# Recurrent layer's last slab: a separate load of the logarithm's table behind the square

## The chip, the cores and the metric

The kernel runs on one core of one Trainium2 chip. The metric is the device time of one execution in microseconds; the median of three runs is given. Engines are named as in the profile: PE is TensorE's matrix multiply and PEld its weight load, DVE is VectorE, ACT is ScalarE, POOL is GpSimd, SP is SyncE, which here issues most DMAs.

## The reference, cut to what matters

Four layers run one after the other on x of 32 sequences of 64 tokens with 256 features: a cross-attention block, two transformer decoder layers, and a recurrent layer of the RWKV kind. The change lies in the last of them. Cut to its second half, that layer computes

```python
outs = scan over 64 steps of:  out = r_t . (u * a + s);  s = a + w_t * s;  a = k_t outer v_t
att  = outs.reshape(b, l, E)
a4   = att.reshape(b, l, 32, 8)                       # 32 heads of 8
m    = mean(a4, -1);  var = mean((a4 - m) ** 2, -1)
att  = ((a4 - m) * rsqrt(var + 1e-5)) * gn_w + gn_b   # group norm over a head
x    = x + att * g @ Wo.T                             # g = silu gate
xn2  = layernorm(x);  sx2 = token_shift(xn2)
rr   = sigmoid((xn2 + sx2 * maa_r) @ ffn_Wr.T)
kk   = square(relu((xn2 + sx2 * maa_k) @ ffn_Wk.T))
x    = x + rr * (kk @ ffn_Wv.T)
```

The reciprocal square root of the group norm is the place of the change.

## The kernel before, in words

All data of the recurrent layer are kept with features on the partitions and tokens along the free axis. The 2048 tokens are cut into eight slabs n = 0 to 7 of four sequences, 256 tokens each (`RB` = 4, `RR` = 256); slab n is half u = n % 2 of group g = n // 2. A slab's work is a list of pieces in three parts, made by `recurrent` (L631):

- first: layer norm and token shift, the five mixes, the projections, the decay, the gate;
- second: the outer products and the scan on VectorE, the sum over keys, then the group norm `norm_a` (L845) and `norm_b` (L855), and the output projection Wo with `to_rows` (L870), whose result `add_to_x` (L214) adds to x;
- third: the feed-forward part: its layer norm (`norm`, L648, through `layernorm_T`, L155), the mixes `xk` and `xr` (L681), `ff_key` (L900: project, then Relu at L903 and Square at L904), the receptance projection `pfr` whose result `done_r` (L906) turns into a tanh (L909), and the value projection `pfv`, whose result `done_v` (L911) multiplies and adds on VectorE (L914, L915) and writes out by DMA (L916).

Each piece has a time written by hand (`FIRST`, `SECOND`, `THIRD`, `ENDS`, L15 to L19), in units of a slab, with slab n shifted by n. `emit` (L93) sorts the pieces of all slabs by these times and calls them, so that the third part of slabs 4, 5 and 6 lies among the second part of slab 7. The program is then ordered for each engine by a scheduler that simulates a timeline (L1268). An instruction can be pinned behind another one by `tc.issue_after`, which `at_once` (L142) uses for runs of matmuls.

The group norm in detail. `norm_a` adds the own term (L847), takes the heads' mean by two matmuls with an averaging matrix into the bank `pgm` (L850), subtracts it on VectorE (L851), and squares on ScalarE into `sq` (L853). `norm_b` takes the mean of the squares by two more matmuls into the bank `pgv` (L859). The power -1/2 is then made on ScalarE as exp(-0.5 ln(v + 1e-5)):

```python
nc.scalar.activation(ps, ps, AF.Ln, bias=tiny[:, 1:2])     # L861
nc.scalar.activation(ps, ps, AF.Exp, scale=-0.5)           # L862
```

and VectorE multiplies with scale and gate (L865, L866). The output projection `pwo` (L875) waits for that, and `add_to_x` (L216) for the projection.

ScalarE evaluates a function from a table, and a set of tables is brought in by an instruction of its own, ACT_TABLE_LOAD. These loads are not written in the kernel: they are put into ScalarE's stream ahead of an activation whose function is not in the set that is there, once the order of the stream is known. They carry the line of the activation that they serve (L861 ahead of the logarithm, L862 ahead of the exponential, L599 and L500 in the transformer layers, L794 in the decay).

The small matrices of the feed-forward part (`pln`, `pst`, `pkk`, `pfr`, `pfv`) lie in PSUM banks with the tag "tp", of which there are two, taken in turn (`BUFS`, L110); a matmul into a bank waits until the reader of what was in it before is done.

Of the kernel before, what the change touches and what calls it, by code (L numbers as in the profile page):

```python
# [33 lines left out]
AF = mybir.ActivationFunctionType  # L34
# [6 lines left out]
NG = 4  # L41
# [57 lines left out]
def tile_xattn_stack(ctx: ExitStack, tc: tile.TileContext, a: dict, out: bass.AP):  # L99
    nc = tc.nc  # L100
# [11 lines left out]
    def bank(name, tag="mm"):  # L112
        return psum.tile([P, 512], FP, tag=tag, name=name, bufs=BUFS[tag])
# [517 lines left out]
    def recurrent(n, pool, c3):  # L631
# [3 lines left out]
        st = {}  # L635
# [9 lines left out]
        def tile_(name, bufs=2, shape=None, p=pool, tag=None):  # L645
            return p.tile(shape or [P, 2, RR], FP, tag=tag or name, name=f"{name}_{t}", bufs=bufs)
# [198 lines left out]
        def norm_a():  # L845
            at = st["at"] = tile_("at")
            nc.vector.tensor_tensor(at, st["own"], st["pa"], ALU.add)  # L847
            ps = bank(f"pgm_{t}", "pc")[:, :RR]
            for c in range(2):
                nc.tensor.matmul(ps, c3["avg"], at[:, c], start=(c == 0), stop=(c == 1))  # L850
            nc.vector.tensor_tensor(at, at, ps.unsqueeze(1).broadcast_to([P, 2, RR]), ALU.subtract)  # L851
            st["sq"] = tile_("sq", 1)
            nc.scalar.activation(st["sq"], at, AF.Square)  # L853

        def norm_b():  # L855
            at, sq = st["at"], st["sq"]
            ps = bank(f"pgv_{t}", "pc")[:, :RR]
            for c in range(2):
                nc.tensor.matmul(ps, c3["avg"], sq[:, c], start=(c == 0), stop=(c == 1))  # L859

            nc.scalar.activation(ps, ps, AF.Ln, bias=tiny[:, 1:2])  # L861
            nc.scalar.activation(ps, ps, AF.Exp, scale=-0.5)  # L862
            gnh = c3["gnh"]
            for c in range(2):
                nc.vector.scalar_tensor_tensor(at[:, c], at[:, c], gnh[:, c : c + 1], ps, ALU.mult, ALU.mult)  # L865
                nc.vector.scalar_tensor_tensor(  # L866
                    at[:, c], at[:, c], gnh[:, 2 + c : 3 + c], st["gt"][:, c], ALU.add, ALU.mult
                )
# [16 lines left out]
        for fn in (spread, outer, scan, read, over_keys):  # L885
            second += [(0.5, lambda fn=fn, e=e: fn(e)) for e in range(2)]
        second += [(0.5, norm_a), (0.5, norm_b)]
        def done_o(ps):
            add_to_x(g, u, ps)
# [58 lines left out]
    with tc.tile_pool(name="lw", bufs=1) as wp, tc.tile_pool(name="lp", bufs=2) as pool:  # L948
# [157 lines left out]
        for i, L in enumerate(("L1", "L2")):  # L1106
            for k in range(2):
                for g in range(NG):
# [5 lines left out]
                    at = (8 + GAP) * i + 4 * k + g  # L1114
# [7 lines left out]
            at = (8 + GAP) * i + MLP  # L1122
# [149 lines left out]
```

## Time and profile before

| what | us |
|---|---|
| median of three runs | 1058.6 |
| the three runs | 1058.6, 1056.49, 1059.2 |
| the profiled execution's own time | 1057.36 |
| its span, from the first to the last instruction | 1055.6 |
| mean granted TensorE clock (of 1) | 0.974 |
| span from 1003 us on: length / TensorE / VectorE / ScalarE busy | 52.6 / 34.7 / 33.4 / 22.7 |
| table loads on ScalarE: number / all together | 49 / 62.9 |
| of these L861 and L862, one each in a slab | 8 and 8 |
| last output's add on VectorE (L915): start | 1051.66 |

How to read it. The share of busy time of an engine is a mean over the whole span. The chain of waits is followed back from the last instruction: at each step to what released it, or to the instruction before it on its engine; "issue" is time in which the engine waited for nothing that the profile shows. Lines of a timeline give start, duration, engine, line of the source, operation, output and inputs with their shapes, a count, and in brackets the idle time ahead of the instruction and who ended it. Starts and durations of neighbours on an engine overlap by some 0.1 us, since instructions are pipelined. Matmuls in float32 appear as two records each. In table-like lines of a group, the numbers behind the bar are busy time in us and the mean in ns of one, then the idle time ahead of it.

The names in the profile have no slab number; by the order of the program, the work from 1024 us on is that of slab 7's group norm, slab 6's layer norm (`xn_fr`, `pln_fr`, `pst_fr`), and the feed-forward parts of slab 4 (`pfr`, `pfv`, `rr` first in time), then 5, 6 and 7.

### The profile page before, as it was taken

The numbers are of one execution on the slowest core, as the hardware profiler recorded it, in microseconds if no ns is written. First come the engines' busy times: TensorE is split into PE (matmuls) and PEld (weight loads), VectorE is DVE, ScalarE is ACT, GpSimd is POOL, SyncE is SP. The second block draws the span as 40 slices with busy tenths as digits, with TensorE's granted clock in tenths as the row PEclk, the third lists the DMA queues.
The fourth block names the chain that finished last, engine by engine and source line by source line (L and its number), as shares of the span: only waits on it lengthen the run. The fifth ranks groups of instructions, "written<-read, shape, count | busy, mean of one in ns | idle before, by whom it ended". The sixth has DMA issues, their size and how long they took to land.

```text
span 1055.6 us, 25954 instructions
## 1 busy us (share of the span) xinstructions
PE 963.1 (91%) x10636; PEld 776.0 (74%) x10636; DVE 741.4 (70%) x1415; ACT 553.4 (52%) x1279; POOL 554.9 (53%) x584
## 2 busy tenths in 40 slices
PE   8999999998999999989999999997979989989757
PEld 4887787776788987967777778875857777666546
DVE  5863778787875646567777865337588786899984
ACT  4744756454466445654554575533545566355244
POOL 4343998798874347578688875130224431243300
PEclk9999999999999999999999999998989999999889
DMA  9300111111101000141101110021321304223401
GB/s 302 112 22 21 42 27 42 42 28 27 32 2 47 1 16 7 58 135 38 41 23 27 27 52 22 11 67 26 92 65 28 90 12 102 70 52 72 100 1 40
DMA packets 45945, 53.36 MB, mean 51 GB/s; under 512 B 16146, under 2 KB 40068, under 8 KB 43780
## 3 DMA queue, kind: packets, MB, share of 16 engines
q1 hardware_dynamic: 40292, 49.60, 17.6%
q10 hardware_dynamic: 5536, 2.12, 0.8%
q8 instruction: 84, 1.38, 0.5%
q14 instruction: 33, 0.27, 0.1%
HBM read 38.83 MB, written 4.21 MB: 41 GB/s over the span
## 4 chain that ended last, share of the span: by engine, by line
PE 43%; DVE 27%; POOL 14%; ACT 7%; issue 3%; DMA 3%; SPq 2%; ACTq 0%; DVEq 0%; POOLq 0%
DVE vb_r L829 7%; PE pf_L2m L205 4%; PE pfo_L1m L205 3%; PE pfo_L2m L613 3%; DVE vb_r L814 3%; POOL s_L2s L481 2%; PE pf_L1m L205 2%; POOL s_L1c L481 2%; POOL s_L2s L485 2%; PE pr L330 2%; SPq L421 2%; DVE x L216 1%; PE pwo_r L875 1%; POOL s_L1c L485 1%; PE pk_r L210 1%
## 5 line engine op out<-in xcount | busy, mean ns | idle before, releaser
L721 POOL TENSOR_TENSOR x_r<-x_r,xn_r 128x512 f32<-128x512 f32 x40 | 60.6, 1530 | 143.1 <-DVE x_r L718 131.8
L829 DVE TENSOR_TENSOR_SCAN vb_r<-wsh,vb_r 128x512 f32<-128x512 f32 x64 | 76.5, 1262 | 14.2 <-ACT wsh L725 14.2
L613 PE MATMUL pfo_L2m<-w_L,hT_L2m 128*128 128x256 f32 x256 | 61.2, 383 | 0.1
L205 PE MATMUL pfo_L1m<-w_L,hT_L1m 128*128 128x256 f32 x384 | 56.0, 292 | 4.7 <-DVE hT_L1m L605 2.1
L205 PE MATMUL pf_L2m<-lnT_L2m,w_L 128*128 128x256 f32 x384 | 55.2, 294 | 2.1 <-ACT hT_L2m L599 2.1
L205 PEld LDWEIGHTS pfo_L1m<-w_L,hT_L1m 128*128 128x128 f32 x384 | 50.5, 195 | 7.8 <-DVE hT_L1m L605 2.9
L205 PEld LDWEIGHTS pf_L2m<-lnT_L2m,w_L 128*128 128x128 f32 x384 | 49.0, 190 | 5.6 <-ACT hT_L2m L599 2.7
L613 PEld LDWEIGHTS pfo_L2m<-w_L,hT_L2m 128*128 128x128 f32 x256 | 47.0, 190 | 7.9 <-issue 1.3
L481 POOL TENSOR_TENSOR s_L2s<-s_L2s,n 128x512 f32<-128x512 f32 x32 | 41.5, 1314 | 20.9 <-DVE s_L2s L476 15.1
L205 PE MATMUL pf_L1m<-lnT_L1m,w_L 128*128 128x256 f32 x384 | 51.6, 287 | 0.1
L481 POOL TENSOR_TENSOR s_L1s<-s_L1s,n 128x512 f32<-128x512 f32 x32 | 40.5, 1282 | 19.7 <-DVE s_L1s L476 19.6
L481 POOL TENSOR_TENSOR s_L1c<-s_L1c,n_L1c 128x512 f32<-128x512 f32 x32 | 41.0, 1302 | 17.0 <-DVE s_L1c L476 16.8
L481 POOL TENSOR_TENSOR s_L2c<-s_L2c,n_L2c 128x512 f32<-128x512 f32 x32 | 40.5, 1286 | 17.6 <-DVE s_L2c L476 17.6
L205 PEld LDWEIGHTS pf_L1m<-lnT_L1m,w_L 128*128 128x128 f32 x384 | 47.8, 191 | 2.0 <-issue 1.2
L605 DVE TENSOR_TENSOR hT_L1m<-hf_L1m,hT_L1m 128x512 fp32r<-128x512 f32 x32 | 29.2, 916 | 24.6 <-POOL hT_L1m L604 24.6
L604 POOL TENSOR_SCALAR hT_L1m<-hf_L1m 128x512 fp32r<-128x512 f32 x32 | 21.4, 671 | 45.6 <-ACT hf_L1m L599 39.6
L599 ACT ACTIVATE hf_L1m<-pf_L1m,b_L 128x256 f32<-128x256 f32 x64 | 26.8, 473 | 29.1 <-PE pf_L1m L205 26.3
L599 ACT ACTIVATE hT_L2m<-pf_L2m,b_L 128x256 f32<-128x256 f32 x64 | 26.6, 472 | 29.0 <-PE pf_L2m L205 28.9
L718 DVE SCALAR_TENSOR_TENSOR x_r<-px_r,vecs,sx_r 128x256 f32<-128x256 f32 x80 | 33.5, 475 | 9.2 <-PE px_r L150 9.2
L300 ACT ACTIVATE att<-pe,nmx 128x256 f32<-128x256 f32 x64 | 29.6, 478 | 19.1 <-DVE nmx L298 16.8
L814 DVE TENSOR_TENSOR vb_r<-vb_r,rT_r 128x2048 f32<-128x2048 f32 x16 | 38.5, 2413 | 0.0
L150 PE MATMUL pa_r<-vb_r,sel 128*32 128x256 f32 x256 | 20.4, 447 | 19.2 <-DVE vb_r L814 19.2
(383 smaller groups left out, 2973.6 us busy)
## 6 DMA issues: line engine op xcount, KB each, us to landing
vb_r<-vd_r SPq DMA_DIRECT2D x16, 1024.0 KB
raw_w_L<-in_L_w_dram SPq DMA_DIRECT2D x3, 1024.0 KB
y<-in_y_dram SPq DMA_DIRECT2D x8, 256.0 KB
x<-in_x_dram SPq DMA_DIRECT2D x8, 256.0 KB
ctxT_L1c<-in_yT_dram SPq DMA_DIRECT2D x4, 512.0 KB
kbd<-kT_L1s SPq DMA_DIRECT2D x64, 32.0 KB
kbd<-kT_L1c SPq DMA_DIRECT2D x64, 32.0 KB
kbd<-kT_L2s SPq DMA_DIRECT2D x64, 32.0 KB
```

The source lines that it names most:

```text
L205: nc.tensor.matmul(ps, sta[x], mov[y], start=(at == 0), stop=(at == n - 1))
L300: nc.scalar.activation(att[:, 2 * h + c, :], pe[:, c, :], AF.Exp, bias=nmx[:, h, c : c + 1], accum_out=rs[:, h, c : c + 1],)
L481: nc.gpsimd.tensor_tensor(s[:, r], s[:, r], n(j).unsqueeze(1).broadcast_to([P, 8, S]), ALU.add)
L485: nc.gpsimd.tensor_tensor(s[:, r], s[:, r], mx[:, hs].unsqueeze(2).broadcast_to([P, 8, S]), ALU.subtract)
L599: nc.scalar.activation(raw[:, i], ps[:, i], AF.Gelu_apprx_tanh, bias=w()["b1"][:, 2 * f2 + i : 2 * f2 + i + 1])
L604: nc.gpsimd.tensor_scalar(h[:, 0], raw, 1.0, 0.0, ALU.mult, ALU.add)
L605: nc.vector.tensor_tensor(h[:, 1], raw, h[:, 0], ALU.subtract)
L613: nc.tensor.matmul(st["ps"][:, v], st["h"][:, f, rows], w2[:, f], start=(f == 0), stop=(f == 7))
L718: nc.vector.scalar_tensor_tensor(d[:, c], banks[m][:, c], vec("L3_maa_stack", 2 * m + c), sx_("x", c), ALU.add, ALU.mult)
L721: nc.gpsimd.tensor_tensor(d, d, st["x"], ALU.add)
L814: nc.vector.tensor_tensor(v, v, x.unsqueeze(1).broadcast_to([P, 4, 2 * RR]), ALU.mult)
L829: nc.vector.tensor_tensor_scan(v[:, d], flat(st["wsh"]), v[:, d], 0.0, ALU.mult, ALU.add)
```

## The change

```diff
@@ norm_a
             st["sq"] = tile_("sq", 1)
-            nc.scalar.activation(st["sq"], at, AF.Square)
+            st["squared"] = nc.scalar.activation(st["sq"], at, AF.Square).ins
 
@@ norm_b
             for c in range(2):
                 nc.tensor.matmul(ps, c3["avg"], sq[:, c], start=(c == 0), stop=(c == 1))
 
+            if n == 2 * NG - 1:
+
+                with tc.issue_after(st["squared"]):
+                    nc.scalar.preload_act_table(AF.Ln)
             nc.scalar.activation(ps, ps, AF.Ln, bias=tiny[:, 1:2])
             nc.scalar.activation(ps, ps, AF.Exp, scale=-0.5)
```

For the last slab only (n = 7), an ACT_TABLE_LOAD of the logarithm's set is written into the kernel, and pinned behind the square of the same slab. Nothing is taken out. Four lines are added ahead of L861, so a line number of the kernel before from L861 on is greater by four in the changed one (the logarithm is L865, the exponential L866, `pwo` L879, the tanh L913); the new load has L864.

The order of ScalarE's stream from that square to that exponential, in the two programs (slab numbers from the program's names):

```
before                                changed
L853 square, slab 7                   L853 square, slab 7
                                      L864 table load
L173 normalise, slab 6, x2            L173 normalise, slab 6, x2
                                      L913 table load
L909 tanh, slab 4                     L913 tanh, slab 4
L861 table load                       L865 table load
L861 logarithm, slab 7                L865 logarithm, slab 7
L862 table load                       L866 table load
L862 exponential, slab 7              L866 exponential, slab 7
```

TensorE's stream differs in one place: in the program before, the four transposes `pln` of slab 6 stand behind the first matmul of slab 7's `pwo`; in the changed one they stand ahead of all four. The other engines have the same instructions in the same order.

## The prediction

> **What bounds the kernel now.** I read the page first, for the engines' shares and the chain that ended last, then that chain in order of time for the last 40 us, then ScalarE (ACT) alone for the same stretch, and last the groups of table loads.
>
> ```profile
> span 1055.6 us, 25954 instructions
> PE 963.1 (91%) x10636; PEld 776.0 (74%) x10636; DVE 741.4 (70%) x1415; ACT 553.4 (52%) x1279; POOL 554.9 (53%) x584
> PE 43%; DVE 27%; POOL 14%; ACT 7%; issue 3%; DMA 3%; SPq 2%; ACTq 0%; DVEq 0%; POOLq 0%
> ```
>
> TensorE is busy for 91% and ScalarE for 52%. That average says nothing of the place of the edit: the last 28 us of the span are a single dependent string of small steps, in which each engine hands on to the next. The chain there:
>
> ```profile
> 1019.57 1.99 PE pwo_r L875 x8
> ...
> 1023.76 1.73 PE pfr_r L875 x8
> 1025.48 1.73 PE pfv_r L875 x8
> 1027.21 0.88 PE pgv_r L859 x4
> 1028.09 0.02 issue
> 1028.11 0.45 ACT pgv_r L861
> 1028.56 0.02 issue
> 1028.58 1.28 ACT L862
> ...
> 1029.87 0.38 ACT pgv_r L862
> ...
> 1031.60 0.70 PE pwo_r L875 x2
> 1032.29 0.44 PE pln_fr L181 x4
> 1032.73 1.31 PE pwo_r L875 x6
> ```
>
> The logarithm of slab 7 (L861, at 1028.11) starts 0.02 us after the matmuls pgv that make its input. What held it is TensorE, and not a table. From there the chain runs through logarithm, the exponential's load, exponential, VectorE, pwo and so on to the end: each microsecond by which the logarithm comes later is one at the end. ScalarE in front of it (start, duration):
>
> ```profile
> 1024.52 0.63 ACT L853 ACTIVATE sq_r<-at_r 128x512 f32<-128x512 f32 x1 [0.32 <-DVE at_r L851]
> 1025.05 1.08 ACT L173 ACTIVATE xn_fr<-x,nmr_fr,rstd_fr 128x256 f32<-128x256 f32 x2
> 1026.04 0.57 ACT L909 ACTIVATE rr_r<-pfr_r 128x512 f32<-128x512 f32 x1
> 1026.63 1.28 ACT L861 ACT_TABLE_LOAD   x1
> 1028.11 0.45 ACT L861 ACTIVATE pgv_r<-pgv_r,tiny 128x256 f32<-128x256 f32 x1 [0.20 <-PE pgv_r L859]
> ```
>
> The square, two normalisations (slab 6), the tanh of slab 4's receptance gate (L909), the logarithm's load. The load ends at 1026.63 + 1.28 = 1027.91, and ScalarE then sits idle for 0.20 us until pgv is there. So the load that the change wants to move is hidden already, with 0.20 us to spare: a perfect move is worth nothing.
>
> **The change part by part.** (1) The edit names one load more. It does not take the old one out, because the tanh stands between the square and the logarithm. In the changed program ScalarE's order is: square, load, normalisation x2, load, tanh, load, logarithm, load, exponential. The normalisations (Identity) run on whatever table is there, as they do in slab 4, where Identities stand between logarithm and exponential with a single load. The tanh does not: it needs its own table back, and the logarithm then needs its own again. So three loads stand where one stood, two more than before. Each costs 1.283 us, in all groups of them:
>
> ```profile
> L861 ACT ACT_TABLE_LOAD x8 | 10.3, 1283 | 2.5 <-DVE x L216 2.4
> L862 ACT ACT_TABLE_LOAD x8 | 10.3, 1283 | 0.1
> ```
>
> Walked forward with gaps of 0.02 us ahead of a load and 0.01 behind it (as around 1028.58): square to 1025.15; load 1025.17 to 1026.45; normalisations 1026.46 to 1027.55 (1.08 to 1.09 for two); load 1027.57 to 1028.85; tanh, whose input has been there since 1025.5, 1028.86 to 1029.45 (mean of that line 0.59); load 1029.48 to 1030.76; logarithm at 1030.77. That is 1030.77 - 1028.11 = 2.66 us late: 2 x 1.28 of loads, some 0.3 of overlaps between neighbours that the loads break up, less the 0.20 of idle time.
>
> The Trainium skill ("ScalarE: Activation LUTs", "What ACT_TABLE_LOAD costs") gives a load 1283 ns, as here, and a drain of about 1380 ns on top, 2.66 us for every switch. The rows do not show that drain: the exponential starts 0.01 us after its load. By that rule two switches would be 5.3 us and the total about 1063.5 us. The same page ("Table sets: the hidden batching unit") tells the author to do all calls of one set before switching, and that speaks against a load placed ahead of a tanh.
>
> (2) What waits behind the delayed tanh. Its bank is that of the next pkk (slab 5), in a pair of banks taken in turn, and pkk lists a wait for ScalarE. Before, pkk followed pgv at once (1028.09); now it waits for the tanh to 1029.45, an idle gap of 1.36 us on TensorE. pkk and the pfr behind it (1.73 us each) then end at about 1033.0. VectorE's L914 (slab 4's output, 1.4 us with L915) waits for the same tanh: 1029.47 to 1030.9, its DMA 2 us later. Both are covered: nothing needs them before the normalised rows reach VectorE, 1030.27 + 2.66 = 1032.93, and pwo, 1031.60 + 2.66 = 1034.26. If that cover were too short, pwo would move by the excess; 1.2 us are to spare.
>
> (3) TensorE's order changes in one place. Before, four transposes pln (0.44 us, slab 6) stood between the first pair and the other six records of pwo, so pwo lasted 1031.60 to 1034.04 = 2.44 us. In the changed program they stand ahead of all of pwo, which then lasts 1.99, as slab 6's own pwo did at 1019.57. That is 0.45 us gained on the chain, if the transposes are done by 1034.26. They need the bank that ScalarE frees with slab 5's first kk (L903), directly behind the exponential: exponential 1032.53 to 1032.90, kk to about 1033.4, transposes to about 1033.95. It fits with 0.3 us to spare. Had they to wait for slab 5's tanh instead (0.63 + 0.60 after kk), they would end at about 1035.2, and pwo would be 0.9 us late. Bounds of this step: -0.45 to +0.9 us; I take -0.45, since kk is the reader of the bank that is next in turn.
>
> All other engines have the same instructions in the same order. Behind pwo the chain has the same waits as before: VectorE's sum, statistics, Pool, and the last feed-forward.
>
> The sum: +2.66 - 0.45 = +2.2 us. The profiled execution took 1057.36 us (span 1055.6 and 1.8 around it), so 1059.6; it was 1.2 us under the median of 1058.6, against which 2.2 more is 1060.8. The three runs shown lie 2.7 us apart (1056.49 to 1059.2), 0.26%. So about 0.3% (3.2 us) is what can be told from no change, and the forecast, +0.21%, lies inside that.
>
> **The rivals.**
> *TensorE's clock falls (slower).* The clock is granted in stretches of 3.41 us:
>
> ```profile
> 198.48:201.89 3.41, 1.72 (x17) 1.00 0.16 39
> 201.89:205.30 3.41, 3.41 (x14) 0.50 0.02 5
> 317.90:321.30 3.40, 2.02 (x75) 1.00 0.09 18
> 321.30:324.70 3.40, 3.40 (x32) 1.00 0.00 0
> ```
>
> The columns are the stretch, its length, TensorE's busy time (instructions), the granted clock, the DMA's share and GB/s. A stretch with 1.72 us busy (an idle gap of 1.69) was followed by one at half clock; one with 2.02 busy (a gap of 1.38) was not. The new gap of 1.36 us, if it falls in one stretch, leaves 2.05 busy: just on the safe side. Were the gap some 0.3 us longer, the next 3.41 us would do half their work, 1.7 us late, with pkk, pfr and part of pwo in them; at most 1.2 of it is absorbed ahead of pwo, else 1.7 arrives. Added: 1.2 to 1.7, total +3.4 to +3.9, 1062.0 to 1062.5. For it: the margin is only 0.3 us and how the stretches lie to the kernel is chance. Against: the 1.38 row.
> The skill ("TensorE: Matmul & The Clock Gate", "Part 1: The HAM clock gate (the “warmup” mystery)") has the half rate only after about a whole idle window of 3.4 us; the row at 198.48 shows it after half of one, and by the page this rival would cost nothing.
>
> *The transposes come late.* The other end of step 3: 2.66 + 0.9 - 0.45 = +3.1 us, 1061.7. For it: three ScalarE instructions stand close behind the exponential. Against: the order of the banks.
>
> *The extra loads cost nothing on the path (equal or faster).* If the repeated loads were skipped because the table is there, or the tanh could move away, the logarithm would again be held by pgv and only the 0.45 of step 3 would remain: 1058.15. This is also the case in which the edit does what it says. For it: only the idle 0.20 us and the new order of pwo. Against: the changed program issues the loads, and each of 49 loads in this trace took 1.28 us, whatever stood ahead of it.
>
> **How the numbers follow.** Forecast (+2.2) 0.65; clock 0.12; late transposes 0.12; free loads 0.11. The forecast is 1.0 us under the bound of 3.2 us and the runs shown scatter by 2.7 in all, so a third of it (0.22) may be read as slower; the clock case gives 0.11 and the late transposes 0.07: slower 0.40. Faster by over 0.3% could only be scatter around the last case: 0.03. Within 0.3%: 0.57. The range: down to 1058.6 the forecast less most of the scatter, and up to 1063.4, the clock case with 0.9 of scatter; outside lie most of the free loads and the far ends of scatter.
>
> **What would show it.** In the changed profile: 51 table loads instead of 49, three of them between slab 7's square and its logarithm; the logarithm 0.01 us behind a load and no longer behind pgv; 6.2 us from the square's start to the logarithm's (before 3.6); pkk 1.3 to 1.4 us after pgv; pwo 1.99 us in one piece, 3.5 us behind the logarithm's start as before; the granted clock at 1.00 up to the end. It would be wrong if loads after a load were shorter, if pwo waited for the transposes, or if the clock fell in the last 25 us.

## The result, and the profile after

| | before | changed |
|---|---|---|
| median of 20 runs each, us | 1059.2 | 1063.16 |
| ratio of times | 1 | 1.0033 (95%: 1.0019 to 1.0048) |
| profiled execution, us | 1057.36 | 1068.0 |
| from the start of slab 7's square to the start of the last add | 27.14 | 29.37 |
| from the span's start to that square | 1024.52 | 1032.88 |

By the ratio the changed kernel is slower by 3.5 us (2.0 to 5.1) in 1059; the two medians lie 3.96 us apart. The stretch that the prediction argued about, from slab 7's square to the end, grew by 29.37 - 27.14 = 2.23 us. The profiled execution of the changed kernel happened to be a long one, and its head (all that comes ahead of the square, where both programs have the same instructions) holds 8.4 us of its 10.6. So times below are counted from the square, with 1032.88 as zero in the changed kernel and 1024.52 in the one before.

The page of the changed kernel, then its groups of table loads (line, engine, operation, count, busy us, mean ns, idle time before):

```profile
span 1066.2 us, 25956 instructions
...
PE 964.8 (90%) x10636; PEld 777.8 (73%) x10636; DVE 745.4 (70%) x1415; ACT 556.2 (52%) x1281; POOL 555.3 (52%) x584
```

```profile
L865 ACT ACT_TABLE_LOAD x8 | 10.3, 1283 | 2.5 <-DVE x L216 2.4
L866 ACT ACT_TABLE_LOAD x8 | 10.3, 1283 | 0.1
...
L864 ACT ACT_TABLE_LOAD x1 | 1.3, 1283 | 0.0
L913 ACT ACT_TABLE_LOAD x1 | 1.3, 1283 | 0.0
```

ScalarE has two instructions more (1281 for 1279), and they are two loads: the explicit one (L864) and one ahead of slab 4's tanh (L913). The logarithm's own load (L865) still stands eight times, once in each slab. ScalarE's timeline of the changed kernel:

```profile
1032.88 0.63 ACT L853 ACTIVATE sq_r<-at_r 128x512 f32<-128x512 f32 x1 [0.32 <-DVE at_r L851]
1033.53 1.28 ACT L864 ACT_TABLE_LOAD   x1
1034.83 1.09 ACT L173 ACTIVATE xn_fr<-x,nmr_fr,rstd_fr 128x256 f32<-128x256 f32 x2
1035.93 1.28 ACT L913 ACT_TABLE_LOAD   x1
1037.23 0.60 ACT L913 ACTIVATE rr_r<-pfr_r 128x512 f32<-128x512 f32 x1
1037.84 1.28 ACT L865 ACT_TABLE_LOAD   x1
1039.14 0.45 ACT L865 ACTIVATE pgv_r<-pgv_r,tiny 128x256 f32<-128x256 f32 x1
```

There is no idle time in it from the square to the logarithm, which starts 6.26 us behind the square (before: 3.59) and directly behind a load: the bracket that named pgv as what it waited for is gone. TensorE at the same time, with the idle time ahead and who ended it in brackets:

```profile
1035.41 1.03 PE L859 MATMUL pgv_r<-sq_r,avg 128*128 128x256 f32 x4
1037.88 1.99 PE L210 MATMUL pkk_r<-xk_r,ffn_Wk 128*128 128x256 f32 x8 [1.44 <-ACT rr_r L913]
...
1041.83 0.66 PE L181 MATMUL pln_fr<-ident,xn_fr 128*128 128x128 f32 x4 [0.23 <-ACT kk_r L907]
1042.62 1.99 PE L879 MATMUL pwo_r<-Wo,at_r 128*128 128x256 f32 x8
```

pgv was ready at its old place, and pkk waits 1.44 us for the tanh. The four transposes pln wait for kk, and pwo stands whole behind them. The last add of the last output, on VectorE, ends the stretch at 1062.25 - 1032.88 = 29.37:

```profile
1062.25 0.69 DVE L919 SCALAR_TENSOR_TENSOR rr_r<-rr_r,x 128x512 f32<-128x512 f32 x1
```

The clock stayed up behind the new gap (stretch, length, TensorE busy and instructions, granted clock, DMA share, GB/s):

```profile
1036.20:1039.61 3.41, 1.97 (x10) 1.00 0.02 5
1039.61:1043.02 3.41, 3.04 (x16) 1.00 0.23 77
```

### The profile page after: what moved, and what is told of

Same layout as the page of the kernel before. It is cut to its first block, busy times and chain, and to the rows that moved or that the text cites. A ratio compares the mean times of both kernels' runs of the same rounds, so it can differ in the third digit from the quotient of the medians.

```text
span 1066.2 us, 25956 instructions
## 1 busy us (share of the span) xinstructions
PE 964.8 (90%) x10636; PEld 777.8 (73%) x10636; DVE 745.4 (70%) x1415; ACT 556.2 (52%) x1281; POOL 555.3 (52%) x584
## 3 DMA queue, kind: packets, MB, share of 16 engines
q10 hardware_dynamic: 5536, 2.12, 0.9%
## 4 chain that ended last, share of the span: by engine, by line
PE 41%; DVE 26%; POOL 14%; ACT 7%; DMA 5%; issue 3%; SPq 2%; DVEq 0%; ACTq 0%; POOLq 0%
DVE vb_r L829 7%; PE pf_L2m L205 4%; PE pfo_L2m L613 3%; DVE vb_r L814 3%; PE pfo_L1m L205 2%; POOL s_L2s L481 2%; PE pf_L1m L205 2%; POOL s_L1c L481 2%; POOL s_L2s L485 2%; PE pr L330 1%; SPq L421 1%; PE pwo_r L879 1%; DVE x L216 1%; POOL s_L1c L485 1%; PE pk_r L210 1%
## 5 line engine op out<-in xcount | busy, mean ns | idle before, releaser
L481 POOL TENSOR_TENSOR s_L1s<-s_L1s,n 128x512 f32<-128x512 f32 x32 | 40.5, 1283 | 20.8 <-DVE s_L1s L476 20.7
```

The costliest lines, as they stand in the source:

```text
L481: nc.gpsimd.tensor_tensor(s[:, r], s[:, r], n(j).unsqueeze(1).broadcast_to([P, 8, S]), ALU.add)
```

## The experiments

All profiles, counted from the start of slab 7's square. "Logarithm" is the start of slab 7's logarithm; "stretch" is from the square to the start of the last output's last add; "head" is the square's place in the span.

| kernel | loads | logarithm | stretch | head | ratio of total, 95% |
|---|---|---|---|---|---|
| before | 49 | 3.59 | 27.14 | 1024.52 | 1 |
| changed | 51 | 6.26 | 29.37 | 1032.88 | 1.0033 (1.0019 to 1.0048) |
| again | 51 | 6.26 | 29.37 | 1024.63 | 1.0016 (0.9995 to 1.0037) |
| again2 | 51 | 6.26 | 29.37 | 1029.25 | 1.0035 (1.0014 to 1.0055) |
| pin_tanh | 49 | 3.60 | 27.14 | 1026.21 | 0.9997 (0.9976 to 1.0018) |
| gate4_copy | 49 | 3.60 | 27.08 | 1021.77 | one run |
| ln_twice | 52 | 7.55 | 31.49 | 1026.10 | one run |
| two_more | 53 | 8.83 | 34.03 | 1024.36 | 1.0063 (1.0041 to 1.0086) |
| pwo_whole | 49 | 3.59 | 26.80 | 1028.41 | one run |
| one_set7 | 49 | 3.60 | 26.81 | 1026.20 | one run |
| nmr_first | 49 | 3.60 | 26.10 | 1023.32 | 1.0003 (0.9985 to 1.0020) |

The stretch was 29.37 us in all three profiles of the changed kernel, whose heads differ by up to 8.25 us. So the stretch is the instrument here, and the total only a check on it.

### pin_tanh: the same load, behind the tanh

```diff
-                with tc.issue_after(st["squared"]):
+                with tc.issue_after(c3["tanh", 4]):
                     nc.scalar.preload_act_table(AF.Ln)
...
-            nc.scalar.activation(st["rr"], ps, AF.Tanh, scale=0.5)
+            c3["tanh", n] = nc.scalar.activation(st["rr"], ps, AF.Tanh, scale=0.5).ins
```

> The same explicit load of the logarithm's table, pinned behind slab 4's tanh in place of slab 7's square, so that no other function stands between it and the logarithm: 49 loads, as before. Theory (the cost is the two loads that the tanh forces): the stretch from slab 7's square to the last add falls back to 27.14 us, total 1.000. Rival (an explicit, pinned load costs by itself): stays at 28 to 29.4. Rival (the changed total comes from a longer head, not from the tail): total still 1.001 or more.

ScalarE of this kernel:

```profile
1027.73 0.57 ACT L913 ACTIVATE rr_r<-pfr_r 128x512 f32<-128x512 f32 x1
1028.33 1.28 ACT L864 ACT_TABLE_LOAD   x1
1029.81 0.45 ACT L865 ACTIVATE pgv_r<-pgv_r,tiny 128x256 f32<-128x256 f32 x1 [0.20 <-PE pgv_r L859]
```

The explicit load now takes the place of the one that was put in (L865 has none of its own), the 0.20 us of idle time in front of the logarithm and the wait for pgv are back, and the stretch is 27.14 to the hundredth. An explicit load costs nothing by itself; its place ahead of the tanh does.

### gate4_copy: no other table between square and logarithm

```diff
-            nc.scalar.activation(st["rr"], ps, AF.Tanh, scale=0.5)
+            nc.scalar.activation(st["rr"], ps, AF.Copy if n == 4 else AF.Tanh, scale=0.5)
```

> The changed kernel with slab 4's tanh replaced by a copy of the same size (the receptance gate of slab 4 is left linear), so that nothing between square and logarithm needs another table: 49 loads, the explicit one right behind the square, as the edit meant it. Theory: the logarithm is held by pgv again, 3.59 us behind the square's start; the stretch from square to last add is 27.14 less what the whole pwo brings. Since pkk and pfr then end at their old place, pwo waits for the transposes behind pfr and gains 0.25 and not 0.45: 26.9 us. Rival (the early load itself delays the string): 28 us or more.

```profile
1021.77 0.63 ACT L853 ACTIVATE sq_r<-at_r 128x512 f32<-128x512 f32 x1 [0.32 <-DVE at_r L851]
1022.42 1.28 ACT L864 ACT_TABLE_LOAD   x1
1023.72 1.09 ACT L173 ACTIVATE xn_fr<-x,nmr_fr,rstd_fr 128x256 f32<-128x256 f32 x2
1024.71 0.57 ACT L913 ACTIVATE rr_r<-pfr_r 128x512 f32<-128x512 f32 x1
1025.37 0.45 ACT L865 ACTIVATE pgv_r<-pgv_r,tiny 128x256 f32<-128x256 f32 x1
```

This is the change working as it is written: one load right behind the square, no other until the logarithm. The logarithm starts 3.60 us behind the square, where it stood before the change. So a load that is placed well is worth nothing at this place, as it had cover already, and the two extra loads of the changed kernel come from the tanh. The stretch is 27.08, not 26.9: pkk starts at 3.57 in place of 3.39, since it waits for the copy (which ends at 3.51, where the tanh before ended at 2.09), and passes that on to the transposes and pwo.

### two_more and ln_twice: what one load costs, and when the clock falls

The edit of two_more; ln_twice is the same without the lines marked.

```diff
                 with tc.issue_after(st["squared"]):
-                    nc.scalar.preload_act_table(AF.Ln)
+                    first = nc.scalar.preload_act_table(AF.Ln).ins
+                with tc.issue_after(first):
+                    first = nc.scalar.preload_act_table(AF.Tanh).ins   # two_more alone
+                with tc.issue_after(first):                            # two_more alone
+                    nc.scalar.preload_act_table(AF.Ln)
```

> The changed kernel with two more table loads (tanh's and the logarithm's set in turn) on ScalarE ahead of slab 4's tanh, 53 in all; TensorE's order at pwo is that of the kernel before. Theory (1.28 us per load, in place of 0.45 gained by the order of pwo): the logarithm 2.57 us later than in the changed kernel, the stretch from square to last add 29.37 + 2.6 + 0.45 = 32.4 us, total 1.0050. TensorE's gap ahead of pkk becomes 4.0 us; if its clock falls after a gap, as the prediction's first rival has it, pkk, pfr or pwo run at half rate for 3.4 us and the stretch is up to 1.5 us longer, 32.5 to 33.9, total up to 1.0064. Rival (loads in a row are cheaper, since a table that is there is not loaded again): 30 to 31, total below 1.004.

> The changed kernel with the explicit load of the logarithm's table written twice, one right behind the other in effect: the second finds its own table in place. 52 loads. Theory (a load costs 1.28 us whatever stands there): tanh and logarithm 1.29 us later than in the changed kernel, the stretch from square to last add 29.37 + 1.29 = 30.66 us if TensorE keeps its clock. TensorE's gap ahead of pkk becomes 2.72 us, 1.0 more than the 1.69 that cost the clock elsewhere; if a stretch of 3.4 us at half rate follows, up to 0.9 us more, 31.6. Rival (the prediction's third: a table that is there is not loaded again): 29.37.

ScalarE of ln_twice, where by the program the load at L866 brings the table that L864 has brought already (only the normalisations run in between):

```profile
1029.15 1.28 ACT L866 ACT_TABLE_LOAD   x1
1030.44 1.28 ACT L915 ACT_TABLE_LOAD   x1
1031.74 0.60 ACT L915 ACTIVATE rr_r<-pfr_r 128x512 f32<-128x512 f32 x1
```

It takes 1.28 us like any other, and the next starts 1.29 us after it. The logarithm comes at 7.55 (1.29 later than in the changed kernel) with one load more and at 8.83 (2.57 later) with two: the price is straight, 1.28 to 1.29 us a load, with no separate drain. In two_more the loads switch between two sets, and they too start 1.29 us apart (3.05, 4.34 and 5.63 behind the square). The Trainium skill ("ScalarE: Activation LUTs", "What ACT_TABLE_LOAD costs") states about 1283 ns for the load, which the rows of both kernels have, and about 1380 ns of drain beside it at a switch to a different set, which they do not have.

The stretches grew by more: 31.49 - 29.37 = 2.12 and 34.03 - 29.37 = 4.66. TensorE's gap ahead of pkk is now 2.73 and 4.02 us, and the clock falls behind it. ln_twice, then two_more:

```profile
1029.38:1032.79 3.41, 0.68 (x4) 1.00 0.00 0
1032.79:1036.20 3.41, 3.41 (x10) 0.50 0.26 82
```

```profile
1027.67:1031.08 3.41, 0.25 (x2) 1.00 0.00 0
1031.08:1034.49 3.41, 2.56 (x6) 0.50 0.09 27
1034.49:1037.91 3.42, 3.42 (x9) 0.50 0.16 55
```

TensorE itself, ln_twice first:

```profile
1032.39 3.42 PE L210 MATMUL pkk_r<-xk_r,ffn_Wk 128*128 128x256 f32 x8 [2.73 <-ACT rr_r L915]
```

```profile
1031.93 3.78 PE L210 MATMUL pkk_r<-xk_r,ffn_Wk 128*128 128x256 f32 x8 [4.02 <-ACT rr_r L917]
1035.51 3.08 PE L883 MATMUL pfr_r<-ffn_Wr,xr_r 128*128 128x256 f32 x8
```

The eight records of pkk take 3.42 and 3.78 us in place of 1.99, and pwo now waits for TensorE's queue: it starts at 11.97 in ln_twice, where ScalarE and VectorE would have let it go at 9.74 + 1.29 = 11.03. That is 0.94 us, and 2.12 - 1.29 = 0.83 of it reaches the end. In two_more the second stretch at half clock follows one that was busy for 2.56 of its 3.41 us; 4.66 - 2.57 = 2.09 is left, of which, as an estimate, 0.45 is the split pwo of this program (step 3 of the prediction) and 1.6 the clock. The expectation (up to 33.9) reckoned with one stretch at half rate and was 0.13 short.

### pwo_whole and one_set7: the other two ways to shorten the string

pwo_whole is the kernel before with slab 7's pwo pinned behind slab 6's transposes (`last_turn[tag]` holds each layer norm's last transpose):

```diff
+                if w == "Wo" and n == 7:
+                    with tc.issue_after(last_turn["fr6"]):
+                        both_rows()
+                else:
+                    both_rows()
```

> The kernel before with one thing of the changed one: the matmuls of slab 7's pwo pinned behind slab 6's four transposes. Theory of the prediction's step 3 in place (0.45 us gained where TensorE has idle time for the transposes): here there is none, since pkk and pfr run up to 6.85 us behind the square's start, so the transposes end at 7.3 and pwo starts 0.2 later than its 7.08 and is 0.45 shorter: the stretch 26.9 us (0.1 to 0.3 under 27.14). Rival (the order is worth its full 0.45 by itself): 26.7. Rival (nothing): 27.14.

one_set7 has this too, and in slab 7 a single table set for logarithm and exponential:

```diff
+                with tc.issue_after(c3["tanh", 4]):
+                    nc.scalar.preload_act_table_set("natural_log_exp_and_others")
```

> In slab 7 one table set that has both logarithm and exponential is loaded, pinned behind slab 4's tanh, so that the exponential needs no load; the load that slab 5's tanh then needs stands behind the exponential and the two instructions of kk. 49 loads. TensorE's pwo is whole as in the changed kernel. Theory (the exponential's load lies on the chain only as far as TensorE is not busy with pkk and pfr): the exponential ends 1.29 us earlier, but pwo cannot start before 7.3 us behind the square, where pfr and the transposes end: the stretch 26.9 us. Rival (all 1.28 us of the load come off the end): 25.4 to 25.9.

ScalarE of one_set7, then its TensorE:

```profile
1029.80 0.45 ACT L867 ACTIVATE pgv_r<-pgv_r,tiny 128x256 f32<-128x256 f32 x1 [0.20 <-PE pgv_r L861]
1030.28 0.37 ACT L868 ACTIVATE pgv_r<-pgv_r 128x256 f32<-128x256 f32 x1
...
1032.80 1.28 ACT L921 ACT_TABLE_LOAD   x1
```

```profile
1031.32 1.89 PE L882 MATMUL pfr_r<-ffn_Wr,xr_r 128*128 128x256 f32 x8
1033.05 0.60 PE L181 MATMUL pln_fr<-ident,xn_fr 128*128 128x128 f32 x4
1033.48 1.89 PE L882 MATMUL pwo_r<-Wo,at_r 128*128 128x256 f32 x8
```

The exponential follows the logarithm at 4.08 in place of 5.35, without a load between. The skill (same page, "Table sets: the hidden batching unit") names this set as one that has both functions, so that the logarithm and then the exponential take one load. It holds here with the set loaded by name; in the kernel before, the pair takes two loads in every slab (8 at L861 and 8 at L862). Yet the stretch is 26.81 with it and 26.80 without it (pwo_whole): TensorE's queue is full of pkk, pfr and transposes, with no idle time between the rows shown, and pwo starts at 7.28 in both. So the whole gain of 0.34 is pwo's order, and the exponential's load, 1.28 us on the chain of the kernel before, is worth nothing once pwo stands behind that queue. The 0.34 itself lies between what was expected (0.1 to 0.3) and the rival's 0.45: pwo starts 0.20 later, as expected (7.28 for 7.08), but takes 1.89 us from its first record's start to its last one's end, where it took 2.43 before, 0.54 less and not 0.45.

### nmr_first: a queue's order instead of a load's place

Beside pwo_whole's pin, slab 6's second mix is made late and behind slab 7's nmr (L170) on VectorE:

```diff
+        def xr():
+            if n == 6 and "mixed" not in st:
+                st["mixed"] = True
+                with tc.issue_after(last_turn["nmr", "fr7"]):
+                    mixed("fx", st["xr"], "L3_ffn_maa_r")
+            return st["xr"]
...
-        third += to_rows(lambda: st["xr"], "ffn_Wr", done_r, "fr")
+        third += to_rows(xr, "ffn_Wr", done_r, "fr")
```

> The kernel before with the whole pwo, and on VectorE slab 6's xr mix (two instructions, 0.8 us) pinned behind the small step nmr of slab 7's last layer norm, which stood behind it. Table loads as before. Theory (what is worth having in these 30 us is the order of the queues, not the place of a load that has cover): nmr, 14.04 us behind the square's start before, comes 0.8 to 1.0 us earlier, and the end 0.5 to 1.1 us with it: the stretch 26.0 to 26.6 us, a total of 0.999 that the scatter of the runs will hide (0.997 to 1.001). Rival (pkk of slab 6, which TensorE takes first, holds the next step): 26.9, as with the whole pwo alone.

VectorE of this kernel:

```profile
1035.64 0.68 DVE L932 SCALAR_TENSOR_TENSOR rr_r<-rr_r,pfv_r 128x512 f32<-128x512 f32 x1
1036.24 0.15 DVE L170 SCALAR_TENSOR_TENSOR nmr_fr<-mv_fr,rstd_fr 128x2 f32<-128x2 f32 x1
1036.31 0.87 DVE L685 SCALAR_TENSOR_TENSOR xr_r<-sx_fr,vecs,xn_fr 128x256 f32<-128x256 f32 x2
```

nmr starts 12.92 us behind the square (before 14.04, pwo_whole 13.70) and the stretch is 26.10, 1.04 shorter than before and 3.27 shorter than changed. Of the 1.04, 0.34 is pwo's order (pwo_whole) and 0.70 that of VectorE's queue. The total, 1.0003 (0.9985 to 1.0020), cannot show 0.1%: better than the kernel before in this stretch, and not told apart from it in time.

### again and again2: the total

> The changed kernel itself, once more. Measured in the two profiles: from the start of slab 7's square to the start of the last add of the last output it is 27.14 us before and 29.37 us changed, +2.23, where the total moved by 1.0033 (1.0019 to 1.0048), +3.5 us (+2.0 to +5.1). Theory (the whole cost lies behind that square): 29.37 again to within 0.05, and a total of 1.0021. Rival (a second cost of about 1.3 us lies ahead of the square): 29.37 again, a total of 1.0033 again, and the start of the square later than before's in every profile of a kernel with this edit.

> The changed kernel a third time, for the total: so far 1.0033 (1.0019 to 1.0048) and 1.0016 (0.9995 to 1.0037) against a stretch from square to last add that was 29.37 us both times, 2.23 longer than before's 27.14, which is 1.0021. Theory (nothing ahead of the square, and the clock keeps full rate behind a gap of 1.44 us): 29.37, total 1.001 to 1.003. Rival (the clock falls in some executions): 30.2 to 31 in this profile, or a total of 1.003 to 1.004 again.

Both stretches are 29.37, with the clock at full rate behind the gap; in each the gap falls whole into one stretch of the clock, with 1.97 us busy, as in the first profile. Over all runs of the three comparisons the mean is 1062.4 us changed (44 runs, standard deviation 2.5) and 1058.9 before (61 runs, 2.5): 3.4 us apart, with a standard error of 0.5 if the runs are independent. The stretch explains 2.23 of that.

## Why the prediction was right, point by point

**What bounds.** Right. The logarithm was held by pgv and not by its load; with the load moved and no tanh in between (gate4_copy) it starts where it did. "Each microsecond by which the logarithm comes later is one at the end" holds for later, and not for earlier: in one_set7 an exponential that comes 1.27 us earlier brings nothing, since pwo then waits for TensorE's queue.

**Step 1, two more loads.** Right, in count and size. The logarithm was forecast 2.66 us late and came 6.26 - 3.59 = 2.67 late. Loads cost 1.28 us each, also where the table is there already (ln_twice), which takes the third rival away.

**Step 2, pkk behind the tanh.** Right: an idle gap of 1.44 us, forecast 1.36. pwo starts at 9.74 behind the square, as forecast (1034.26 - 1024.52).

**Step 3, pwo whole.** Right: the transposes wait for kk (the profile names it), end ahead of pwo (0.13 us ahead, at 8.95 + 0.66 = 9.61, where 0.3 was forecast), and from pwo's start to the sum behind it (L216) pass 2.03 us in place of 2.47, so 0.44 gained, forecast 0.45. The second rival, transposes that wait for the next tanh, did not happen. The gain rests on idle time in front of pwo: without it (pwo_whole) the same order brought 0.34.

**The sum.** 2.67 - 0.44 = 2.23, forecast 2.2.

**The clock.** The first rival did not happen in the three profiles of the changed kernel: a stretch with 1.97 us busy kept the clock. Its mechanism and price are shown by ln_twice: with a gap of 2.73 us, the clock halved and 0.83 us more reached the end. The prediction added 1.2 to 1.7 for this case, which its own terms do not give: 1.7 us late, of which at most 1.2 is absorbed, is 0.5 to 1.7, and the 0.83 lies there. The three profiles do not rule the case out for the executions that were not profiled.

**The total.** Its range held, but with some luck. The median of 1063.16 lies only 0.24 us under the upper bound of 1063.4, and nearer to the clock case (1062.0 to 1062.5) than to the forecast's 1060.8, though the clock did not fall in any of the three profiles: the total alone would have pointed to the wrong cause. The prediction also gave the larger chance, 0.57, to a change within 0.3%; the measured ratio of 1.0033 lies just beyond that, where it gave 0.40. The interval (1.0019 to 1.0048) contains the likeliest case, 1.0021. The term that is too small is not one of the sum's: it is 1.2 us (3.4 - 2.2) that the stretch does not have. They do not lie behind the last add, since from there to the end of the span pass 3.9 us in every profile. So they lie ahead of the square, or in executions whose last stretch differs from the profiled ones, or they are scatter.

For scatter speak the heads. Six profiles with the load behind the square have 1021.8 to 1032.9, mean 1026.5; five without it have 1023.3 to 1028.4, mean 1025.7; up to the square all have the same computing instructions in the same order on every engine. two_more has the same edit, a stretch 6.89 longer than before's, and a total 6.7 longer, which leaves nothing for the head, though its interval (4.3 to 9.1) has room for 1.2 us. Against scatter stand two of three comparisons at 1.0033 and 1.0035, and that equal instructions do not make equal heads: from slab 0's square to slab 7's pass 275.0 to 275.2 us in eight profiles, but 275.8 to 275.9 in pwo_whole, one_set7 and nmr_first, the three with pwo's pin, for a reason that is not known. The changed kernel's three profiles have 275.0 to 275.1 there and the kernel before 275.2, so the 1.2 us do not lie in that part of them. What makes them stays open.

## What to carry to other kernels

A table load written by hand takes the automatic one away only if no function of another set runs between it and the function that it serves; otherwise it buys two loads more, 1.28 us each, so read the finished order of the queue and not the place in the source. Look first at who ends the wait in front of the function: where that is another engine, as here, a load has cover already and the best move is worth nothing. In this string of small steps at the end of a kernel the order of two queues (which of two instructions an engine takes first) was worth 1.04 us, where a load moved to a good place (pin_tanh) or left out (one_set7 against pwo_whole) was worth nothing.

## What the runs showed of the hardware

- Loading a table that is already active takes the full 1.28 us (L866 in ln_twice).
- The clock kept full rate behind a stretch of 3.41 us with 1.97 busy and fell to half behind ones with 0.68 and 0.25. Busy time alone does not decide it: in the kernel before, the stretch from 812.90 with 1.41 us busy kept it, where the one with 1.72 shown in the prediction lost it. It stayed at half for a second stretch where the first was busy for only 2.56 of 3.41 us (two_more), and came back after one that was busy throughout (ln_twice).
- The last 29.37 us of the changed kernel repeated to 0.01 us in its three profiles, and pin_tanh's 27.14 us equal those of the kernel before, while the 1020 us ahead, with the same instructions, varied by 11 us between the eleven profiles.
